# New orders for all engines, one buffer of v and five of x, in a two-layer graph attention kernel

## The chip, the cores and the metric

The kernel runs on one core of a Trainium2 chip. A core has five engines that run side by side, each through its own list of instructions in order: TensorE (PE; its weight loads are shown apart, as PEld), VectorE (DVE), ScalarE (ACT), GpSimd (POOL) and SyncE (SP), which here issues all transfers (DMA). An instruction that needs another engine's result waits on a semaphore, and everything behind it in its engine's list waits too. The metric is the time of one execution on the device, in microseconds (us). The median of three runs of the kernel before is 3153.78 us (3152.27 to 3154.47).

## The reference

The input is 64 graphs of 256 nodes, each node with 512 features, and an adjacency matrix per graph. Two layers follow each other. Both normalise x over the features, apply a relu, compute an attention over the edges of the graph, and add the result to x:

```python
h = jnp.maximum(_layernorm(x, axis=-1), 0.0)
x = x + _L0_gnn_ref(h, adj, ...)     # 8 heads of 64
h = jnp.maximum(_layernorm(x, axis=-1), 0.0)
x = x + _L1_gnn_ref(h, adj, ...)     # one head
```

Layer 0 is attention with queries, keys and values, and a gate:

```python
q, k, v = x @ Wq.T, x @ Wk.T, x @ Wv.T                      # split in 8 heads
scores = where(adj != 0, q @ k.T / 8, -inf)
c = softmax(scores) @ v
gate = sigmoid(concatenate([c, x]) @ Wg.T + bg)
return gate * x + (1 - gate) * c
```

Layer 1 takes its scores from two vectors: `Wh = h @ W`, `e = leaky_relu(Wh @ a1 + (Wh @ a2).T)`, a softmax over the edges, and `elu(softmax(e) @ Wh)`. All is float32.

## The kernel before

Every graph passes through some 190 named steps, and each step issues a few instructions on one engine. The order is written out by hand: `PLAN` gives each step a time within the graph (`sc.0@12.5`), graph g is shifted by g times `ROUND` = 48, `MOVED` holds tables of their own for graphs 0, 1, 2 and the last three, and `ONCE` places the work on the weights. All steps of all graphs are sorted by these times, and the instructions are issued in that order; each engine keeps it. The times themselves decide nothing but the order. Because a graph's steps stretch from about -25 to 161, four graphs are in work at once, and one round of 48 on each engine mixes steps of graph g (queries, keys, values, scores), g-1 (weighing, gate), g-2 and g-3 (layer 1).

Names that the change and the prediction touch, with their lines:

- `product` (L368 on PE, L381 and L385 for the sums): each of the products qk, v, z (the gate) and wh (layer 1) is done by a scheme with seven half-size products instead of eight. Steps `.1` to `.7` are the matmuls, `.u1` to `.u3` partial sums, `.c00` to `.c11` the four quadrants of the result. They need sums of halves of the left side (`Sh`, `Sg`, `Sc`, `S1`, on POOL, L352).
- `sc.0`, `sc.1` (L565): scores of four heads each, two heads at a time on 64 rows of PE; four PSUM banks each. `max.hji` (DVE, L575) adds the mask, writes `e` and its row extreme `low`, and so empties the bank; `exp` (ACT, L585) and `scale` follow, then `turn` (L607), `send`, `fetch`: the transposition of e goes through DRAM.
- `we.hj` (L625) weighs v with e, two heads side by side, into the banks pc; `cT.h` (ACT, L634) copies pc out.
- `po.t` (L802): the product of layer 1. Its bank is read by `pos.t` (ACT, L822), then `neg.t` (DVE, L816); `xn`, `elu` and `add` finish the graph.
- `nm0`, `again` (ACT, L436): the normalising relus; `th`, `sh`, `fh`: the transposition of h through DRAM (DVE L444, SP L452 and L459). Graphs 0 and 1 transpose h on PE instead.
- `w1` in `ONCE`: the two transfers of the weights of layer 1 (L303).

PSUM has 8 banks in one pool (L250). A tile takes a bank that an earlier tile has left, and its first matmul waits until the readers of that tile are done. The order of the steps decides which bank that is. SBUF pools hold a fixed number of buffers for each kind of tile, and work the same way:

```python
    sb = {tag: pool(tag, bufs) for tag, bufs in {
        "x": 4, "mask": 3, "hT": 3, "S": 3, "qk": 2, "v": 2, "wh": 1, "e": 5,
        "cT": 1, "z": 2, "h": 2, "tmp": 5, "U": 3,
    }.items()}
```

Of the kernel before, what the change touches and what calls it, by code (L numbers as in the profile page):

```python
# [23 lines left out]
load@-25.517 st0.0@-25.362 st0.1@-25.032 edges@-22.334 root0@-21.913 nb0@-21.901 nm0.0@-21.307 nm0.1@-20.126  # L24
th.0@-17.618 th.1@-17.305 sh@-14.322 fh@-6.377 Sh.0@-3.038 qk.1@-2.257 Sh.1@-2.212 qk.6@-0.012 v.1@1.071
qk.u1@1.807 qk.u2@2.34 qk.2@2.869 Sh.2@3.73 qk.7@4.792 mask@4.893 qk.c00@6.08 qk.5@6.215 qk.u3@6.435 Sh.3@6.863
qk.c11@7.713 qk.4@8.038 qk.c10@8.845 v.6@9.888 qk.3@10.508 sc.0@12.5 v.u1@13.047 v.u2@13.932 max.000@14.256
max.001@14.568 exp.000@15.12 exp.001@15.307 rec.00@16.501 scale.001@16.56 qk.c01@17.137 max.010@17.753
turn.001@18.015 max.011@18.139 scale.000@18.256 sc.1@18.495 v.7@18.547 v.5@19.32 v.2@19.814 max.101@19.887
exp.010@20.123 exp.011@20.389 max.111@20.411 v.u3@20.681 v.c11@20.959 exp.101@21.371 exp.111@21.858  # L30
max.110@22.149 max.100@22.173 v.3@22.179 v.4@22.277 exp.110@22.423 rec.11@23.42 v.c10@24.24 v.c00@24.916
turn.000@26.369 rec.01@28.756 v.c01@31.638 scale.010@31.798 exp.100@32.951 send.00@33.353 rec.10@35.481
scale.100@38.106 fetch.00@38.826 scale.110@39.168 scale.111@39.248 scale.101@41.535 turn.100@42.016
turn.101@42.558 send.10@43.507 scale.011@43.509 turn.011@44.888 turn.010@45.765 send.01@45.995 Sg.2@46.166
turn.110@47.124 turn.111@49.33 send.11@52.01 fetch.01@56.797 fetch.11@59.033 we.00@61.926 Sg.0@62.715
fetch.10@63.663 we.01@64.269 we.10@64.517 we.11@65.623 cT.1@65.931 cT.0@67.935 tc.0@68.178 tc.1@68.862
z.1@70.621 Sg.1@71.204 again.0@71.805 Sc.0@72.846 sc_c@73.436 again.1@74.487 Sc.1@76.35 fc@76.652 z.6@77.432
Sc.3@77.753 Sg.3@79.038 z.u1@80.986 Sc.2@81.017 z.u2@83.459 plus.0@83.493 z.5@83.895 z.7@84.755 plus.1@85.174
diff.1@85.992 z.u3@87.161 z.c11@88.054 z.u2b@88.325 z.2@89.486 z.c00@89.717 z.c11b@89.726 z.3@89.799 z.4@90.441
tanh.11@90.924 z.c01@91.769 tanh.01@95.639 z.c10@96.01 z.c10b@97.905 tanh.10@98.145 mix.1@98.236 res.1@98.964  # L40
diff.0@99.559 tanh.00@99.951 mix.0@100.406 st1.1@100.781 res.0@100.798 st1.0@100.966 root1@101.973 nb1@102.977
nm1.0@103.141 nm1.1@103.718 th1.0@103.809 th1.1@103.955 sh1@112.184 fh1@115.308 S1.0@115.907 wh.1@116.663
S1.1@117.265 wh.6@118.302 wh.u1@118.466 wh.5@121.753 wh.u2@122.654 S1.2@123.088 S1.3@123.832 wh.7@124.6
wh.2@126.678 wh.u3@127.794 wh.c11@128.831 wh.3@129.585 wh.4@129.976 wh.c01@130.035 ej@130.677 wh.c00@131.651
wh.c10@132.05 lo.0@132.707 lo.1@132.844 lk@133.374 gm@134.11 gx.0@134.576 gx.1@135.087 tg@136.647 gr@138.907
sg@139.411 fg@148.441 po.1@152.197 po.0@152.604 pos.1@152.634 neg.1@152.713 xn.1@153.592 elu.1@153.6
neg.0@154.07 pos.0@156.444 xn.0@157.095 add.1@157.968 elu.0@158.19 add.0@158.822 store.1@161.344 store.0@161.344
# [3 lines left out]
load@-66.492 st0.0@-62.166 st0.1@-41.873 nb0@-40.496 nm0.0@-38.867 nm0.1@-38.355 th.1@-34.404 Sh.0@-26.584  # L51
qk.1@-25.431 edges@-18.94 Sh.1@-17.462 Sh.2@-16.454 qk.u1@-10.175 qk.2@-9.152 qk.c00@-7.78 qk.6@-5.72
qk.u2@-3.448 qk.5@-2.78 mask@0.57 qk.7@1.243 Sh.3@1.626 v.1@2.076 qk.u3@3.139 v.6@4.324 qk.c11@4.336 qk.4@5.375
v.u1@5.993 qk.c10@6.112 qk.3@6.393 Sg.0@7.009 v.u2@7.919 sc.0@8.357 qk.c01@9.423 max.001@12.509 max.000@12.592
exp.001@13.04 sc.1@13.629 max.011@13.907 max.010@14.682 exp.000@15.376 v.2@15.579 rec.00@16.911 v.7@17.36
scale.000@18.711 exp.011@19.032 max.101@19.061 max.110@19.132 turn.000@19.238 exp.010@20.325 rec.01@21.098
scale.001@21.597 v.5@22.024 scale.011@22.79 scale.010@23.067 turn.001@24.046 exp.101@25.554 v.u3@26.692
v.4@27.162 turn.011@27.308 again.1@27.619 max.100@27.777 turn.010@32.196 exp.100@32.343 rec.10@32.984
exp.110@33.128 max.111@34.114 exp.111@34.131 v.c11@35.258 v.c10@35.534 v.3@35.908 scale.100@37.307
turn.100@37.416 send.00@37.59 send.01@37.594 fetch.00@37.81 rec.11@39.483 scale.101@40.086 scale.111@40.147  # L60
turn.101@40.354 scale.110@40.455 Sg.1@40.682 turn.111@40.713 turn.110@41.59 v.c00@45.064 send.10@46.347
send.11@47.204 v.c01@48.602 fetch.01@49.506 fetch.10@51.661 fetch.11@54.488 we.00@60.762 we.01@61.54
we.10@61.569 we.11@63.173 cT.0@64.565 cT.1@64.842 tc.1@66.783 tc.0@67.555 Sc.0@69.612 Sg.3@70.908 sc_c@72.721
z.1@72.817 Sc.1@74.782 Sg.2@74.799 Sc.2@75.418 z.5@78.409 z.u1@78.601 z.6@80.632 z.2@81.279 z.u2@81.896
fc@82.244 again.0@83.023 Sc.3@83.211 z.7@83.889 z.u3@85.445 diff.1@85.474 z.c11@85.865 z.4@86.808 z.c10@87.745
diff.0@87.746 z.c00@87.868 z.c11b@88.24 tanh.11@89.515 z.c10b@90.556 z.3@90.697 tanh.10@90.804 z.u2b@91.332
plus.1@91.418 mix.1@91.555 tanh.00@93.686 res.1@93.921 st1.1@94.842 z.c01@95.935 tanh.01@97.013 plus.0@97.295
mix.0@97.955 res.0@99.045 st1.0@99.639 root1@101.517 nb1@104.33 nm1.1@105.445 nm1.0@105.781 th1.1@106.103
th1.0@106.886 sh1@109.588 fh1@113.042 S1.2@115.324 S1.0@118.555 S1.1@119.128 wh.1@119.447 wh.u1@120.614
wh.5@121.547 wh.6@123.717 wh.2@124.548 wh.u2@125.134 S1.3@125.305 wh.c00@126.073 wh.7@126.229 wh.u3@126.984  # L70
wh.c11@127.33 wh.3@127.662 wh.c01@128.416 wh.4@128.924 ej@129.658 wh.c10@130.963 lo.0@132.107 lo.1@133.497
lk@133.677 gm@134.909 gx.0@135.769 gx.1@136.316 tg@137.119 gr@142.324 sg@144.148 fg@150.305 po.1@152.131
po.0@152.865 neg.1@153.296 pos.1@153.813 xn.1@154.051 elu.1@154.34 neg.0@154.926 add.1@155.869 pos.0@156.073
xn.0@157.112 elu.0@158.192 add.0@159.655 store.1@162.725
""",
    1: """
load@-53.598 st0.0@-44.732 st0.1@-42.689 root0@-41.915 nb0@-40.574 nm0.0@-36.709 nm0.1@-22.87 th.1@-21.253
Sh.2@-20.954 qk.1@-19.381 edges@-18.368 Sh.0@-16.578 Sh.1@-15.935 v.1@-15.77 mask@-15.703 qk.6@-13.279
qk.u1@-10.861 v.6@-8.864 qk.u2@-7.508 qk.5@-5.489 qk.7@-4.754 qk.2@-3.858 qk.c00@1.72 qk.u3@5.331 qk.c11@7.207
Sh.3@7.326 qk.4@7.838 qk.c10@8.486 qk.3@8.97 sc.0@9.079 max.001@9.977 exp.001@10.528 v.u1@11.082 max.000@12.255  # L80
v.u2@12.364 exp.000@13.461 max.011@14.196 max.010@15.765 qk.c01@15.794 sc.1@16.565 rec.00@17.993
scale.000@18.895 scale.001@19.223 v.2@19.942 v.7@20.191 turn.000@23.213 v.5@24.104 turn.001@24.94 send.00@25.481
v.u3@25.507 max.101@26.024 v.4@26.782 v.c11@26.961 v.3@28.971 exp.011@29.35 exp.010@29.396 exp.101@29.983
rec.01@30.852 max.110@30.882 max.100@31.75 Sg.0@32.268 max.111@32.42 exp.100@32.663 v.c01@33.021 exp.110@33.03
exp.111@33.081 rec.10@34.808 rec.11@35.041 v.c10@35.764 scale.011@36.086 scale.010@36.5 scale.111@37.128
turn.010@37.67 scale.100@37.935 scale.110@37.969 v.c00@38.069 Sg.2@38.586 turn.011@38.709 scale.101@39.08
turn.100@39.547 turn.101@40.024 send.01@40.421 turn.111@42.041 turn.110@42.176 fetch.00@42.3 send.11@45.118
fetch.01@48.751 again.0@54.727 again.1@58.028 send.10@59.369 fetch.11@60.182 we.01@60.839 fetch.10@61.056
we.00@64.361 we.10@64.363 we.11@64.622 cT.1@65.84 Sg.1@66.919 cT.0@67.49 tc.1@69.264 tc.0@69.429 z.1@69.839
sc_c@71.013 Sc.0@75.071 Sc.1@75.381 fc@75.545 Sc.3@75.836 z.6@78.559 z.u1@80.518 z.u2@80.535 Sc.2@80.727  # L90
z.2@81.066 z.7@82.757 diff.0@82.831 z.u2b@85.217 z.5@85.437 Sg.3@85.608 z.u3@85.949 z.4@86.212 plus.1@86.287
z.c00@88.083 z.c11@88.484 z.c10@89.655 z.3@90.713 plus.0@91.852 z.c11b@92.08 z.c01@93.718 z.c10b@93.892
tanh.00@95.111 diff.1@96.325 tanh.10@96.948 tanh.11@97.047 tanh.01@98.456 mix.1@100.033 res.1@100.15
mix.0@101.437 st1.1@101.796 res.0@102.261 st1.0@102.536 root1@103.086 nb1@104.102 nm1.0@104.132 th1.0@104.221
# [818 lines left out]
```

## Time and profile before

| | |
|---|---|
| median of three runs | 3153.78 us |
| profiled execution, its own time | 3155.37 us |
| its span on the core | 3153.3 us |
| PE busy | 3123.9 us, 99% |
| DVE, ACT, POOL busy | 77%, 47%, 58% |
| transfers | 593 MB, 188 GB/s |
| one round in the steady stretch (from the transposes of `ej` to the next) | 48.46 us |

The profile is one execution. It names groups of instructions by line and by tiles (out<-in), with their busy time, the mean duration of one, and the idle time of the engine in front of them with what ended it. The timeline merges instructions of a kind that follow each other: the start, the time from the first start to the last end, and the number of instructions; in brackets the idle time in front. A float32 matmul appears as two records. Matmuls overlap, so that the time of a group is better read from its start to the start of the next.

### The profile page before, as it was taken

The numbers are of one execution on the slowest core, as the hardware profiler recorded it, in microseconds if no ns is written. First come the engines' busy times: TensorE is split into PE (matmuls) and PEld (weight loads), VectorE is DVE, ScalarE is ACT, GpSimd is POOL, SyncE is SP. The second block draws the span as 40 slices with busy tenths as digits, with TensorE's granted clock in tenths as the row PEclk, the third lists the DMA queues.
The fourth block names the chain that finished last, engine by engine and source line by source line (L and its number), as shares of the span: only waits on it lengthen the run. The fifth ranks groups of instructions, "written<-read, shape, count | busy, mean of one in ns | idle before, by whom it ended". The sixth has DMA issues, their size and how long they took to land.

```text
span 3153.3 us, 61657 instructions
## 1 busy us (share of the span) xinstructions
PE 3123.9 (99%) x19668; PEld 2729.8 (87%) x19668; DVE 2435.7 (77%) x6310; ACT 1471.4 (47%) x4039; POOL 1836.1 (58%) x2502
## 2 busy tenths in 40 slices
PE   8999999999999999999999999999999999999997
PEld 7888888888888888888888888888888888888886
DVE  7787777777777777777777777777777777777875
ACT  4445445454454454444544544445445444454443
POOL 4566565565665655656656556566565565565654
PEclk9999999999999999999999999999999999999999
DMA  7677777777777777777777777777777777777662
GB/s 218 183 193 187 190 196 189 189 190 192 196 185 189 197 187 188 193 190 196 185 190 194 188 186 197 188 195 186 190 195 186 185 200 188 195 184 194 185 177 86
DMA packets 1107155, 593.19 MB, mean 188 GB/s; under 512 B 687632, under 2 KB 1032720, under 8 KB 1106832
## 3 DMA queue, kind: packets, MB, share of 16 engines
q1 hardware_dynamic: 1106832, 589.25, 72.3%
q8 instruction: 158, 2.59, 0.4%
q14 instruction: 165, 1.35, 0.1%
HBM read 306.45 MB, written 282.59 MB: 187 GB/s over the span
## 4 chain that ended last, share of the span: by engine, by line
PE 95%; DMA 1%; DVE 1%; SPq 1%; POOL 1%; issue 0%; ACT 0%; DVEq 0%; POOLq 0%; ACTq 0%
PE pmb_qk L368 10%; PE pmb_z L368 10%; PE ps L565 8%; PE pma_qk L368 7%; PE pmc_qk L368 7%; PE pc L625 7%; PE pma_z L368 7%; PE po L802 7%; PE pmc_z L368 7%; PE pmb_v L368 5%; PE pmb_wh L368 5%; PE pma_wh L368 3%; PE pmc_wh L368 3%; PE pma_v L368 3%; PE pmc_v L368 3%; PE pe L746 0%
## 5 line engine op out<-in xcount | busy, mean ns | idle before, releaser
L585 ACT ACTIVATE e<-e,low 128x256 f32<-128x256 f32 x1024 | 507.0, 500 | 98.9 <-DVE low L575 89.5
L601 POOL TENSOR_SCALAR e<-e,rec 128x256 f32<-128x256 f32 x768 | 383.6, 516 | 122.3 <-DVE rec L592 122.1
L841 POOL TENSOR_TENSOR x<-x,pos 128x512 f32<-128x512 f32 x126 | 160.9, 1277 | 468.5 <-DVE pos L833 468.5
L575 DVE CUSTOM_DVE_ANT_0 e<-ps,mask 128x256 f32<-128x256 f32 x1024 | 375.2, 414 | 9.7 <-PE ps L565 9.6
L607 DVE STREAM_TRANSPOSE eb<-e 128x512 f32<-128x512 f32 x512 | 345.5, 693 | 8.8 <-ACT e L599 1.2
L436 ACT ACTIVATE h<-x,nb_l,rs_l 128x512 f32<-128x512 f32 x256 | 195.0, 808 | 292.7 <-DVE nb_l L431 266.3
L565 PE MATMUL ps<-qk 64*128 64x256 f32 x2048 | 279.9, 392 | 0.4 <-DVE low L575 0.4
L426 POOL TENSOR_TENSOR rs_l<-ve_l,mhalf 128x2 f32<-128x2 f32 (+1 forms) x129 | 90.6, 702 | 297.1 <-DVE ve_l L422 269.2
L565 PEld LDWEIGHTS ps<-qk 64*128 64x128 f32 x2048 | 204.1, 186 | 57.8 <-DVE low L575 23.1
L802 PE MATMUL po<-wh,egT 128*128 128x256 f32 x1024 | 237.3, 384 | 3.2 <-ACT egT L784 2.9
L625 PE MATMUL pc<-eT,v 128*64 128x256 f32 x2048 | 235.6, 382 | 1.9 <-DMA eT<-there_e 1.8
L802 PEld LDWEIGHTS po<-wh,egT 128*128 128x128 f32 x1024 | 192.5, 193 | 29.8 <-ACT egT L784 3.5
L625 PEld LDWEIGHTS pc<-eT,v 128*64 128x64 f32 x2048 | 141.5, 137 | 88.0 <-issue 22.7
L352 POOL TENSOR_TENSOR S<-h1T 128x256 f32<-128x256 f32 x128 | 93.7, 732 | 202.9 <-DMA h1T<-there_h 126.9
L816 DVE TENSOR_SCALAR neg<-po,rec 128x512 f32<-128x512 f32 x128 | 95.7, 748 | 132.5 <-ACT pos L822 129.6
L585 ACT ACTIVATION_READ_ACCUMULATOR e<-e,low 128x1 f32 x1024 | 195.0, 190 | 0.0
L768 ACT ACTIVATE eg<-eg,nm 128x256 f32<-128x256 f32 x128 | 64.0, 500 | 274.3 <-DVE nm L762 274.3
L822 ACT ACTIVATE pos<-po,rec 128x512 f32<-128x512 f32 x128 | 88.0, 687 | 210.6 <-issue 118.1
L444 DVE STREAM_TRANSPOSE h<-h 128x512 f32<-128x512 f32 x248 | 172.0, 701 | 8.7 <-ACT h L436 3.3
L415 DVE BATCH_NORM_STATS2 bs_l<-x 128x6 f32<-128x512 f32 x256 | 174.4, 681 | 3.8 <-DMA x<-in_x_dram 3.4
L381 DVE TENSOR_TENSOR wh<-pmc_wh,u_wh 128x257 f32<-128x257 f32 x128 | 54.5, 426 | 148.5 <-PE pmc_wh L368 146.4
L673 POOL TENSOR_TENSOR d<-d,c 128x512 f32<-128x512 f32 x128 | 164.4, 1285 | 0.0
(152 smaller groups left out, 8265.6 us busy)
## 6 DMA issues: line engine op xcount, KB each, us to landing
there_e<-eb SPq DMA_DIRECT2D x256, 512.0 KB, 3.3
eT<-there_e SPq DMA_DIRECT2D x1024, 128.0 KB, 3.5
there_h<-h SPq DMA_DIRECT2D x496, 128.0 KB, 3.4
there_c<-cb SPq DMA_DIRECT2D x64, 512.0 KB, 2.9
c<-there_c SPq DMA_DIRECT2D x256, 128.0 KB, 2.9
x<-in_x_dram SPq DMA_DIRECT2D x63, 512.0 KB, 4.3
out_dram<-x SPq DMA_DIRECT2D x63, 512.0 KB, 3.2
hT<-there_h SPq DMA_DIRECT2D x248, 128.0 KB, 3.2
```

The source lines that it names most:

```text
L368: nc.tensor.matmul(s[name, key][(slice(None), *cols)], lhsT, rhs, start=first and i == 0, stop=last and i == len(mms) - 1, skip_group_chec ...
L415: nc.vector.bn_stats(bs, s["x"][:, t, :])
L436: nc.scalar.activation(out, s["x"][:, t, :], AF.Relu, bias=s["nb", layer][:, t:t + 1], scale=s["rs", layer][:, t:t + 1])
L444: nc.vector.transpose(h, h)
L565: nc.tensor.matmul(s["ps", half, jj, i][:, t, :], qk[r:r + DK, 0, jj, t * P:(t + 1) * P], qk[r:r + DK, 1, jj, :], start=True, stop=True,)
L575: nc.vector.tensor_tensor_reduce(e[:, i, t, :], s["ps", half, jj, i][:, t, :], s["mask"][:, t, :], -SCALE, HUGE, ALU.add, ALU.min, accum_o ...
L585: nc.scalar.activation(e, e, AF.Exp, bias=s["low", half][:, jj, i, t:t + 1], scale=-1.0, accum_out=sums[:, jj, i, t:t + 1])
L601: nc.gpsimd.tensor_scalar(e, e, rec, 1.0, ALU.mult, ALU.mult)
L607: nc.vector.transpose(eb[:, :, 4 * i:4 * i + 4, :].rearrange("p b n c -> p n b c"), e)
L625: nc.tensor.matmul(pc[i * DK:(i + 1) * DK, jj, :].rearrange("p (t a c) -> p t a c", t=NT, c=32), s["v"][:, kc, hd * DK:(hd + 1) * DK], s[" ...
L673: nc.gpsimd.tensor_tensor(d, d, s["c"][t], ALU.subtract)
L802: nc.tensor.matmul(po[:, n, :], s["egT"][:, t, kc, :], to_wh(s, g, kc, n)[:, :HH], start=(kc, n) == (0, 0), stop=(kc, n) == (NT - 1, 1), s ...
```

## The change

The times in `PLAN`, in the six tables of `MOVED` and in `ONCE` are all rewritten, so the order of the steps is another one on every engine; no step is added or taken away. The pool of v has one buffer in place of two, that of x five in place of four.

On PE, a steady round before has the order qk.4, po.1, po.0, v.6, qk.3, sc.0, we.00, we.01, we.10, we.11, sc.1, v.7, v.5, v.2, wh.1 and so on. After, it is qk.4, po.0, qk.3, v.7, v.2, po.1, sc.0, we.01, we.00, we.10, we.11, sc.1, v.3, v.4, wh.1. On DVE, around the scores: before max.000, max.001, rec.00, qk.c01, max.010, turn.001, max.011, max.101, tc.0; after neg.0, qk.c01, nb0, elu.0, neg.1, max.011, max.010, th.1, v.u3, elu.1, max.000, v.c11, th.0, max.001, max.110. On ACT: before xn.0, exp.000, exp.001, cT.1, cT.0, exp.010, exp.011; after pos.1, xn.1, nm0.1, again.0, nm0.0, cT.0, exp.010, cT.1, exp.000, exp.011.

```diff
 PLAN = """
-load@-25.517 st0.0@-25.362 st0.1@-25.032 edges@-22.334 root0@-21.913 nb0@-21.901 nm0.0@-21.307 nm0.1@-20.126
...
-qk.c11@7.713 qk.4@8.038 qk.c10@8.845 v.6@9.888 qk.3@10.508 sc.0@12.5 v.u1@13.047 v.u2@13.932 max.000@14.256
-max.001@14.568 exp.000@15.12 exp.001@15.307 rec.00@16.501 scale.001@16.56 qk.c01@17.137 max.010@17.753
-turn.001@18.015 max.011@18.139 scale.000@18.256 sc.1@18.495 v.7@18.547 v.5@19.32 v.2@19.814 max.101@19.887
...
-sg@139.411 fg@148.441 po.1@152.197 po.0@152.604 pos.1@152.634 neg.1@152.713 xn.1@153.592 elu.1@153.6
...
+load@-50.672 st0.0@-48.955 st0.1@-47.821 root0@-38.184 nb0@-37.123 nm0.1@-29.56 nm0.0@-28.012 th.1@-27.761
...
+v.7@10.9 v.2@10.953 qk.c00@12.201 sc.0@14.892 max.011@16.85 max.010@18.632 v.u3@21.472 exp.010@22.747
+max.000@23.034 v.c11@23.409 max.001@24.188 sc.1@24.213 exp.000@24.365 exp.011@24.661 v.3@24.788 max.110@24.806
...
+lk@135.599 gm@135.616 gx.1@140.75 gx.0@141.02 tg@141.763 sg@143.83 gr@152.036 fg@153.077 po.0@153.781
+pos.0@153.792 neg.0@153.922 xn.0@156.41 elu.0@157.474 po.1@158.645 add.0@158.767 pos.1@159.243 neg.1@160.27
...
 ONCE = """
-wgc@10.917 wgh@19.432 sumgc.0@42.007 sumgc.2@42.137 sumgc.1@42.313 sumgh.0@47.029 sumgh.2@53.384 sumgh.1@54.715
-sumgc.3@55.21 small@64.212 sumgh.3@73.845 w1@84.687 edge.20@91.004 edge.30@93.277 edge.21@97.801 edge.31@97.88
...
+sumgc.3@67.553 sumgc.2@67.566 w1@71.651 edge.10@73.258 sumgh.3@73.871 edge.01@74.38 edge.00@75.742
...
-        "x": 4, "mask": 3, "hT": 3, "S": 3, "qk": 2, "v": 2, "wh": 1, "e": 5,
+        "x": 5, "mask": 3, "hT": 3, "S": 3, "qk": 2, "v": 1, "wh": 1, "e": 5,
```

On SP, the head had fetch.11/0, load/2, sc_c/0, send.00/1, edges/2, fc/0, sh/2, w1, fh/2 (step/graph); after, load/2 comes in the first transfers, and the order is fetch.01/0, w1, sh/2, fh/2, sc_c/0, fc/0. In the steady round the last fetch of e, fetch.11, now follows sh1 of the graph before.

## The prediction

> **What bounds the kernel now.** I read the page first, then the waits by engine, then the timeline of one round in the steady stretch, then the timeline of the first 100 us. The engine table says that TensorE (PE) is busy for 99% of the span, so no engine that gets faster can help unless PE itself stands still somewhere.
>
> ```profile
> PE 3123.9 (99%) x19668; PEld 2729.8 (87%) x19668; DVE 2435.7 (77%) x6310; ACT 1471.4 (47%) x4039; POOL 1836.1 (58%) x2502
> L565 PEld LDWEIGHTS ps<-qk 64*128 64x128 f32 x2048 | 204.1, 186 | 57.8 <-DVE low L575 23.1
> ```
>
> The row to see is the second. PE's matmul row hides short waits, because matmuls overlap; the weight loader (PEld) does not. It stood 23.1 us before the score matmuls, until VectorE (DVE) had written `low`. The list of waits says in how many pieces, and what else PE waited for:
>
> ```profile
> PEld ps L565 <- DVE low L575: 23.1, 59, 0.6
> PE pma_qk L368 <- DMA hT<-there_h: 5.2, 1, 5.2
> PE ptr L782 <- ACT eg L768: 3.5, 1, 3.5
> ```
>
> 59 waits in 64 graphs: one per round, 0.39 us each. The other two are single waits, one in the head, one in the tail. Now one steady round, all engines:
>
> ```profile
> 1640.34 3.63 PE L802 MATMUL po<-wh,egT 128*128 128x256 f32 x16
> 1642.32 0.69 ACT L822 ACTIVATE pos<-po,rec 128x512 f32<-128x512 f32 x1 [2.10 <-issue]
> 1643.04 0.75 DVE L816 TENSOR_SCALAR neg<-po,rec 128x512 f32<-128x512 f32 x1 [2.08 <-ACT pos L822]
> 1643.83 0.63 ACT L826 ACTIVATE neg<-neg 128x512 f32<-128x512 f32 x1 [0.82 <-DVE neg L816]
> ...
> 1646.54 2.00 PE L565 MATMUL ps<-qk 64*128 64x256 f32 x16
> ...
> 1648.47 3.67 PE L625 MATMUL pc<-eT,v 128*64 128x256 f32 x32
> ...
> 1652.07 2.01 PEld L565 LDWEIGHTS ps<-qk 64*128 64x128 f32 x16 [0.39 <-DVE low L575]
> 1652.07 2.41 PE L565 MATMUL ps<-qk 64*128 64x256 f32 x16
> 1652.19 1.07 ACT L634 COPY cT<-pc 128x512 f32<-128x512 f32 x2 [1.65 <-PE pc L625]
> ```
>
> The first group of 16 score matmuls (sc.0) takes 2.00 us, the second (sc.1, the same work) 2.41. sc.1 needs four PSUM banks; the last one is that of max.011, which DVE empties last (its two reductions start at 1652.55 and 1652.87). From its start to that of the next group, sc.0 takes 1.93 us and sc.1 2.34: 0.41 us lost. That the round pays it in full can be seen early on: the two rounds where sc.1 starts at 198.82 and 247.00 lose 0.13 and 0.20 there, and last 48.18 and 48.25 us; the steady ones lose 0.41 and last 48.46. In the head:
>
> ```profile
> 73.16 1.03 PE L368 MATMUL pmc_z<-wgc_sb,Sc 128*128 128x256 f32 x4
> 79.41 2.05 PE L368 MATMUL pma_qk<-hT,wq_sb 128*128 128x128 f32 x8 [5.23 <-DMA hT<-there_h]
> 81.25 1.92 PE L368 MATMUL pma_qk<-hT,wk_sb 128*128 128x128 f32 x8
> 82.96 1.25 PE L368 MATMUL pma_v<-wv_sb,hT 128*128 128x256 f32 x4
> ```
>
> hT of graph 2 comes 5.23 us late: the two halves of W1 (w1, issued at 66.57) stand in SP's queue between that graph's `sh` and `fh`, and land 8.5 and 9.9 us after issue. After the wait PE runs at about half speed for 16 matmuls: 82.96 - 79.41 = 3.55 us, against 2 x 0.89 for the same in any later round, so 1.8 more.
>
> **The change, part by part.** The work is the same, matmul for matmul, and PE changes between the score, weighing and full-width forms about as often (262 changes in the order as built, 261 before), so PE's own sum moves by nothing. What can move is its waiting.
>
> *sc.1 (the main term).* In the built order sc.1's four banks are now those emptied by max.010, cT.0 (the copy of the first half of pc), max.000 and cT.1; max.011 and max.010 come first on DVE, and max.001's bank is not needed before wh.1, 3.6 us later. So the last bank hangs on ScalarE (ACT). I follow that chain with the rows above, from T, the start of the weighing matmuls. po.1 now stands directly ahead of sc.0. po's last matmul starts 0.22 + 0.09 + 1.93 = 2.24 before T and takes 0.38, so po.1 ends at T-1.86. After po, pos starts 0.09 later and takes 0.69; neg starts 0.03 later and takes 0.75; its exponential starts 0.04 later: T-0.27. ACT then issues, start to start: that exponential 0.54 (0.636 less 0.09 overlap), three normalising relus at 0.72 (0.81 less 0.09), cT.0 at 0.48, exp.010's two halves at 0.49: cT.1 starts at T+3.89 (pc is done at T+3.7, so ACT is what is late), takes 0.59, and a load follows its releaser by 0.05: T+4.53. sc.1 starts at T+3.60, so that load stands 0.93 after the group's start. In the rounds named above this load stood at 1.00, 1.07 and 1.28 after the start and cost 0.13, 0.20 and 0.41: cost = lateness past 0.87. So 0.06 us is left of 0.41. The other banks have more room: cT.0 ends at T+3.0 for a use at T+3.6; max.000 ends after max.011, max.010 (4 x 0.345), th.1 0.62, v.u3 0.33, elu.1 0.62 and 2 x 0.345 at T+3.7, for a load at T+4.36. Bounds: nothing left (0), or as much as now (0.41). I take 0.06 over 58 rounds, 3.5 us: the gain is 23.1 - 3.5 = 19.6.
>
> *The bank of pc's first half* is now the one of po.1, the group just before sc.0. By the same chain neg.1 ends at T-0.31: 0.3 us to spare, no cost. In front of neg.1 on DVE stand elu.0 and, through the buffer that neg reuses, add.0 on POOL (1.28): po.0, pos.0, neg.0, its exponential, elu.0 and add.0 take 0.09 + 0.69 + 0.03 + 0.75 + 0.04 + 0.63 + 0.70 + 1.28 = 4.2 us after po.0 ends, and neg.1 can start no earlier than 6.0 after it (qk.3, v.7, v.2 and po.1 on PE: 1.79 + 2 x 0.86 + 1.73 = 5.2, and pos.1): 1.8 to spare, some 1 us if DVE's qk.c01 (0.66) gets in between. Bounds: 0 to 0.7 us per round, if one DVE operation of 0.70 gets in front.
>
> *One buffer of v.* The first write of the next v (v.c11, 0.41) now has to wait for the last weighing matmul, about T+3.7; DVE comes to it behind max.000 at T+3.7, so it waits for nothing. Queued behind it are th.0 and max.001, whose bank is wanted 1.9 us after max.001 ends (T+5.4 against T+7.3). Cost 0, bounds 0 and 0.34 per round (one v copy less its overlap). The Trainium skill, "Trainium Kernel Development and Optimization", section Best Practices, says to double-buffer for performance, and so speaks against this part; going by it, that upper bound would be booked, 0.34 x 60 = 20 us, and would eat the whole gain. The row behind it, 1.9 us of cover, decides for me.
>
> *A fifth x* lets load and the statistics run a graph earlier (before, x is issued at 1652.70, takes 4.25 us to land and is read at 1658.23): 0, nothing that PE waits for hangs on x in the steady stretch.
>
> *SP's queue.* The last fetch of eT now stands behind sh1, four issues of 0.74 = 3.0 us. Before, the last fetch is issued at 1688.6, lands 3.5 later and is used at 1698.6: 6.5 spare, of which 3.5 are left. sh and fh move ahead likewise. Cost 0; upper bound one late fetch, some 0.5 us a round.
>
> *POOL and the sums.* Sg, Sc, S1, Sh move ahead of the products that read them; PE waits for POOL only in the tail now (0.6), so 0 either way.
>
> *Head.* w1 is issued ahead of graph 2's sh, right behind graph 0's last fetch, about 47 us; by its own rows it has landed by 57, and sh and fh of graph 2 no longer have it between them: their 3.4 and 3.2 us to landing fit before 74.0, where PE came to wait. The 5.2 and the 1.8 us go: 7.0 (bounds 0 and 7). Late next would be graph 2's first sums on POOL, two of 0.76 after the landing.
>
> *New starts and ends.* The orders of graphs 0 to 2 and 61 to 63 are all new. Such rounds now show single bank waits of 0.6 and 0.9 us (near 147 and 152), and the tail 12 us of waits that follow from the chain of the last graph (softmax, transposition, product), which is no shorter after. I book +3, between -3 and +8.
>
> Sum: 19.6 + 7.0 - 3 = 23.6 us less. The profiled execution took 3155.37 (span 3153.3 and 2.1 around it), 1.6 above the median of 3153.78; its 23.6 taken from the median give **3130**.
>
> **Rivals.** (1) *The wait moves instead of going*: the ACT chain ends 0.2 to 0.35 later than worked out (one of the relus held, or exp.010 later), and sc.1 keeps 0.25 to 0.41. For it: the chain is ten operations long with 0.06 missing. Against: each has a steady duration. Gain 23.1 - 58 x (0.25 to 0.41), so 0 to 9, and 4 from head and edges: 3141 to 3150. (2) *Slower*: neg.1 on DVE ends later than T, because something of 0.70 stands before it or add.0 is late. Every 0.1 us beyond the 0.3 spare costs 0.1 at pc and, through its exponential and ACT, another 0.1 at sc.1: 11.6 us in 58 rounds. It decides from about 0.2 beyond the spare; with a whole DVE operation (0.4 beyond) the sum is 23.6 - 46, so 23 slower: 3177. For it: po has been moved right up to sc.0, where before v.6 and qk.3 stood between (2.7 us). Against: nothing in DVE's order stands between. (3) *The wait never cost anything*, the round being bound elsewhere: against it stand the three round lengths; only the head's 7 less 3 would be left, 3150. (4) *All goes, and the edges gain 3*: 3153.8 - 23.1 - 7 - 3 = 3121.
>
> **How the numbers follow.** Forecast 0.55, its own range 3122 to 3138; (4) 0.14; (1) 0.18; (2) 0.08; (3) 0.05. Leaving out the slower case and the upper end of (1) and (3) gives 3118 to 3148. What a measurement of this kernel can tell from no change is 0.2%, 6.3 us: faster by more is below 3147.5, which is the forecast, (4) and most of (1): 0.84. Within: the rest of (1), most of (3): 0.09. Slower: 0.07.
>
> **What would show it.** Right: sc.1 within 0.1 us of sc.0, PEld's wait for `low` gone, rounds of 48.1 us, no wait for hT in the head. Wrong: PEld waiting before ps for ACT cT, or before pc for DVE neg; rounds of 48.4 or more; or new waits for eT and hT in the steady stretch.

## The result and the profile after

The changed kernel takes **3135.73 us** (median of 4 runs, 3133.86 to 3136.5) against 3153.62 of the kernel before in the same job: a ratio of 0.9943, 95% interval 0.9926 to 0.996. The forecast of 3130 lay 5.7 below, and the time is inside the forecast's own range of 3122 to 3138. The profiled execution took 3136.5, span 3134.63, 18.6 less than the 3153.26 of before. Line numbers are one higher than before from the pools on (L565 is now L566).

The page of the kernel after, engine table and costliest groups:

```profile
PE 3104.0 (99%) x19668; PEld 2708.9 (86%) x19668; DVE 2465.1 (79%) x6310; ACT 1458.2 (47%) x4039; POOL 1818.2 (58%) x2502
L566 PE MATMUL ps<-qk 64*128 64x256 f32 x2048 | 257.7, 390 | 0.5 <-ACT neg L827 0.5
L566 PEld LDWEIGHTS ps<-qk 64*128 64x128 f32 x2048 | 192.0, 186 | 60.0 <-DVE low L576 22.9
```

The same group of matmuls on the page of the kernel before, a row that the prediction does not show:

```profile
L565 PE MATMUL ps<-qk 64*128 64x256 f32 x2048 | 279.9, 392 | 0.4 <-DVE low L575 0.4
```

Here is the first surprise. The third row of the first fence still says 22.9 us of waiting for `low`, where the prediction led with 23.1 and expected 3.5 to be left. By that row nothing has happened. But PE's *busy* time on the same matmuls fell from 279.9 to 257.7, by 22.2 us. The loss that the change removed stood in the busy column. The list of PEld's waits after the change shows what the idle row is (columns: what was waited for, us in total, times, longest):

```profile
PEld ps L566 <- DVE low L576: 22.9, 60, 0.5
PEld ps L566 <- issue: 20.3, 61, 0.4
PEld pmc_v L369 <- DVE low L576: 19.2, 58, 0.3
PEld pc L626 <- DVE neg L817: 18.6, 56, 0.3
```

In this kernel every entry into another form of matmul (two heads on 64 rows for `ps`, two on 64 columns for `pc`, full width for `pmc_v`) shows a gap of 0.33 to 0.39 us on the weight loader, once a round, whatever releaser is named, `issue` (no releaser) included; between groups of the same form it is 0.03. It goes with the change of form, and the name beside it is merely that of the last semaphore. Its size is not the same everywhere: the entry into sc.0 shows 0.12 in the kernel before, where qk.3 stands ahead of it with matmuls of 128 columns, and 0.33 after, where po.1 stands there with 256.

One steady round after the change, timeline of all engines (start, duration, engine):

```profile
1639.59 1.60 PEld L566 LDWEIGHTS ps<-qk 64*128 64x128 f32 x16 [0.33 <-issue]
1639.59 2.00 PE L566 MATMUL ps<-qk 64*128 64x256 f32 x16
1639.70 0.69 ACT L823 ACTIVATE pos<-po,rec 128x512 f32<-128x512 f32 x1 [2.85 <-PE po L803]
1640.49 0.75 DVE L817 TENSOR_SCALAR neg<-po,rec 128x512 f32<-128x512 f32 x1 [2.89 <-ACT pos L823]
1641.27 0.63 ACT L827 ACTIVATE neg<-neg 128x512 f32<-128x512 f32 x1 [0.89 <-DVE neg L817]
...
1641.52 3.67 PE L626 MATMUL pc<-eT,v 128*64 128x256 f32 x32
1643.93 0.57 ACT L635 COPY cT<-pc 128x512 f32<-128x512 f32 x1
1645.12 1.61 PEld L566 LDWEIGHTS ps<-qk 64*128 64x128 f32 x16 [0.39 <-DVE low L576]
1645.12 2.02 PE L566 MATMUL ps<-qk 64*128 64x256 f32 x16
1645.39 0.57 ACT L635 COPY cT<-pc 128x512 f32<-128x512 f32 x1
```

sc.1 (1645.12) lasts 2.02 and not 2.41, though the 0.39 of idle time in front of it is exactly that of before. From its start to the start of the next group it takes 1.944 us in the median round (before: 2.337; sc.0: 1.927): 0.017 is left of 0.41, where the forecast left 0.06. With T = 1641.52 the chain falls nearly where the prediction put it: pos at T-1.82 (put at T-1.77), neg at T-1.03 (T-1.05), its exponential at T-0.25 (T-0.27), cT.0 at T+2.41 (T+2.43), cT.1 at T+3.87 (T+3.89).

Where the 18.6 us of span come from, measured between the starts of step `ej`, one per round:

| stretch | before | after | difference | forecast |
|---|---|---|---|---|
| start to first ej | 118.86 | 113.83 | -5.0 | -7.0 |
| rounds 1 to 4 | 47.8, 48.18, 48.25, 48.46 | 48.95, 46.32, 48.05, **55.42** | +6.05 | +3 for all starts and ends |
| 53 steady rounds | 48.46 each | 48.07 each | -20.8 | -19.6 (for 58 rounds) |
| last six rounds, last ej to end | | | +1.1 | in the +3 |

### The profile page after: what moved, and what is told of

The parts are those of the page before. It is cut to its first block, busy times and chain, and to the rows that moved or that the text cites. A ratio compares the mean times of both kernels' runs of the same rounds, so it can differ in the third digit from the quotient of the medians.

```text
span 3134.6 us, 61537 instructions
## 1 busy us (share of the span) xinstructions
PE 3104.0 (99%) x19668; PEld 2708.9 (86%) x19668; DVE 2465.1 (79%) x6310; ACT 1458.2 (47%) x4039; POOL 1818.2 (58%) x2502
## 4 chain that ended last, share of the span: by engine, by line
PE 96%; DVE 2%; DMA 1%; issue 0%; ACT 0%; SPq 0%; POOL 0%; DVEq 0%; ACTq 0%
PE pmb_qk L369 11%; PE pmb_z L369 10%; PE ps L566 8%; PE pc L626 7%; PE pmc_qk L369 7%; PE po L803 7%; PE pma_z L369 7%; PE pma_qk L369 7%; PE pmc_z L369 7%; PE pmb_wh L369 5%; PE pmb_v L369 5%; PE pmc_v L369 4%; PE pmc_wh L369 3%; PE pma_wh L369 3%; PE pma_v L369 3%
## 5 line engine op out<-in xcount | busy, mean ns | idle before, releaser
L602 POOL TENSOR_SCALAR e<-e,rec 128x256 f32<-128x256 f32 x768 | 354.7, 482 | 24.9 <-DVE rec L593 20.7
L608 DVE STREAM_TRANSPOSE eb<-e 128x512 f32<-128x512 f32 x512 | 336.1, 684 | 6.4 <-DMA there_e<-eb 5.7
L566 PE MATMUL ps<-qk 64*128 64x256 f32 x2048 | 257.7, 390 | 0.5 <-ACT neg L827 0.5
L803 PE MATMUL po<-wh,egT 128*128 128x256 f32 x1024 | 245.8, 383 | 4.3 <-DMA egT<-there_g 2.5
L566 PEld LDWEIGHTS ps<-qk 64*128 64x128 f32 x2048 | 192.0, 186 | 60.0 <-DVE low L576 22.9
L684 ACT ACTIVATE z<-z 128x256 f32<-128x256 f32 x256 | 93.5, 409 | 309.5 <-POOL z L391 190.3
L803 PEld LDWEIGHTS po<-wh,egT 128*128 128x128 f32 x1024 | 192.0, 193 | 30.2 <-DMA egT<-there_g 2.9
L626 PEld LDWEIGHTS pc<-eT,v 128*64 128x64 f32 x2048 | 141.1, 137 | 86.3 <-DVE neg L817 18.6
L679 POOL TENSOR_TENSOR x<-x,c 128x512 f32<-128x512 f32 x128 | 200.3, 1565 | 0.0
L391 POOL TENSOR_TENSOR z<-z,bias 128x256 f32<-128x256 f32 x128 | 90.6, 727 | 168.3 <-DVE z L382 168.2
```

Of the source, the lines that this page charges most:

```text
L566: nc.tensor.matmul(s["ps", half, jj, i][:, t, :], qk[r:r + DK, 0, jj, t * P:(t + 1) * P], qk[r:r + DK, 1, jj, :], start=True, stop=True,)
L602: nc.gpsimd.tensor_scalar(e, e, rec, 1.0, ALU.mult, ALU.mult)
L608: nc.vector.transpose(eb[:, :, 4 * i:4 * i + 4, :].rearrange("p b n c -> p n b c"), e)
L626: nc.tensor.matmul(pc[i * DK:(i + 1) * DK, jj, :].rearrange("p (t a c) -> p t a c", t=NT, c=32), s["v"][:, kc, hd * DK:(hd + 1) * DK], s[" ...
L679: nc.gpsimd.tensor_tensor(xt, xt, s["c"][t], ALU.add)
L803: nc.tensor.matmul(po[:, n, :], s["egT"][:, t, kc, :], to_wh(s, g, kc, n)[:, :HH], start=(kc, n) == (0, 0), stop=(kc, n) == (NT - 1, 1), s ...
```

## The experiments

**One swap on DVE, nothing else.** In the kernel before, `turn.001`, a transposition of e for the heads before, stood ahead of `max.011`, whose bank sc.1 waits for. One number of PLAN is changed:

```diff
-turn.001@18.015 max.011@18.139
+turn.001@18.2 max.011@18.139
```

> The kernel before, with one entry of the plan moved: turn.001 goes behind max.011 on DVE, so that max.011, which empties the last bank of sc.1, ends 0.62 us earlier. Theory A (the steady gain is the 0.41 us that sc.1 loses inside its group, and the round pays it in full): sc.1 shrinks from 2.34 to about 1.93 us start to start, the round from 48.46 to 48.05, the time by about 0.41 x 57 = 23 us, to about 3130. Theory B (the gain of the changed kernel needs its whole new order, the sums further ahead on POOL and DVE): the round stays above 48.3 and the time above 3145. Side test: if the 23.1 us that the list of waits put on DVE low is that loss, its row goes; if that row is the gap at the entry of the group, it stays at some 20 us under one name or another.

Measured: 3134.84 (3132.06 to 3135.58), ratio 0.9938 [0.9924, 0.9953]. sc.1 takes 1.928 us, the steady rounds are 48.05. The page of this run beside its list of PEld's waits:

```profile
L565 PE MATMUL ps<-qk 64*128 64x256 f32 x2048 | 256.5, 389 | 0.2 <-DVE low L575 0.2
```

```profile
PEld ps L565 <- DVE low L575: 22.5, 58, 0.6
```

So one transposition of 0.7 us in the wrong place in DVE's list was the whole loss inside sc.1, and moving it alone gives as much time as the rewriting of all orders. It also settles the reading of the rows: the loss is gone and the idle row stays at 22.5. The time lies 4.8 above theory A's 3130; eight rounds of this run last 0.14 to 1.4 us longer than 48.05, 4.5 us in all. PE's timeline in the longest of them:

```profile
684.73 1.10 PE L368 MATMUL pma_wh<-w_sb,h1T 128*128 128x257 f32 x4 [1.14 <-DMA h1T<-there_h]
```

In six of the eight, PE's weight loader stands 0.3 to 1.5 us before this first product of layer 1 and starts 0.1 to 0.2 us after h1T, the transposed input, has landed (the list of waits puts these six down to ACT, once more a name only); in the other two it stands 0.4 and 0.6 us before the next product, for POOL's sums of h1T. In the steady rounds h1T lands 0.1 to 1.6 us ahead of that product in the kernel before, and 3.0 to 4.7 us ahead in the changed kernel, whose 53 steady rounds have none of these waits. That margin is what the new order has over the one swap. Why h1T comes late in just these rounds stays open.

**The pools alone.** In the kernel before:

```diff
-        "x": 4, "mask": 3, "hT": 3, "S": 3, "qk": 2, "v": 2, "wh": 1, "e": 5,
+        "x": 5, "mask": 3, "hT": 3, "S": 3, "qk": 2, "v": 1, "wh": 1, "e": 5,
```

> The kernel before with the pools alone changed: one buffer of v, five of x, all orders as before. Theory A (v's first write comes behind the last weighing matmul on DVE anyway): no difference, 3152 to 3156, rounds of 48.46. Rival (the second buffer of v is worth something): every round longer by up to 0.34 us, up to 3175.

Measured: 3154.58 (3152.4 to 3156.53), ratio 1.0002 [0.9993, 1.0012], rounds of 48.46 as before. Giving up a buffer of v costs nothing in this order, and neither does a fifth x bring anything. The prediction set against this part the advice to double-buffer (Trainium skill, "Trainium Kernel Development and Optimization", Best Practices) and an upper bound of 20 us. The page gives as its aim to "Overlap DMA with compute"; v is written by DVE and ACT and not by a transfer, so this run does not test the page's advice. It shows that the 20 us are not there. The other way round, two buffers of v within the changed order, was not tried.

**The price of a late bank.** In the changed kernel, `exp.011` is put ahead of cT.1 on ACT, so that sc.1's last bank comes 0.98 us later:

```diff
-max.001@24.188 sc.1@24.213 exp.000@24.365 exp.011@24.661
+max.001@24.188 sc.1@24.213 exp.000@24.365 exp.011@23.3
```

> The changed kernel with exp.011 ahead of cT.1 on ACT (one entry of PLAN). Tests the price by which the forecast was made: cost of sc.1 = lateness of its last bank's load past 0.87 us after the group's start. Both halves of exp.011 take 0.98 us of ACT, so cT.1, and with it that load, comes 0.98 later, at about 1.87 after the start. Theory A: sc.1 from start to next start 1.94 + about 0.98 = 2.92 us, rounds of 49.0 instead of 48.07, 55 rounds: about +54, 3190 (3183 to 3197). Theory B (PE's group can be held without the round paying, or the held matmuls are overtaken): less than half, below 3162.

Measured: 3187.99 (3187.45 to 3192.18), 52 more than the changed kernel. The timeline around sc.1, and the waits of PEld in this run:

```profile
1671.13 1.16 PEld L566 LDWEIGHTS ps<-qk 64*128 64x128 f32 x10 [0.39 <-DVE low L576]
1671.13 1.56 PE L566 MATMUL ps<-qk 64*128 64x256 f32 x10
...
1672.39 0.57 ACT L635 COPY cT<-pc 128x512 f32<-128x512 f32 x1
...
1673.01 0.73 PEld L566 LDWEIGHTS ps<-qk 64*128 64x128 f32 x6 [0.72 <-ACT cT L635]
1673.01 1.13 PE L566 MATMUL ps<-qk 64*128 64x256 f32 x6 [0.31 <-ACT cT L635]
```

```profile
PEld ps L566 <- ACT cT L635: 39.5, 57, 0.7
PEld ps L566 <- DVE low L576: 22.8, 59, 0.5
PEld ps L566 <- issue: 20.7, 62, 0.4
```

The late load stands 1.87 us after the group's start; less 0.87 that is 1.00, and sc.1 takes 2.930, 1.00 more than sc.0. In the changed kernel the same load stands at 0.888, and 0.017 is lost. The price "lateness past 0.87" holds over a span of 1 us, and the round pays it in full (49.05 against 48.07). A real wait looks like this: a row of its own that was not there before, of 0.69 us x 57, inside the group, while the 22.8 beside it has not moved. And even here the row understates: 39.5 us of idle time where these groups got 55 us longer (178.5 against 123.5 in sum), because the load of the other head of the pair goes on alone meanwhile and counts as busy.

**The slower rival, on purpose.** In the changed kernel `neg.1` goes behind the two reductions of `max.011` on DVE:

```diff
-po.1@158.645 add.0@158.767 pos.1@159.243 neg.1@160.27
+po.1@158.645 add.0@158.767 pos.1@159.243 neg.1@161.0
```

> The changed kernel with neg.1 behind max.011 on DVE (one entry of PLAN): the slower rival's mechanism made on purpose. neg.1 starts at about 1642.33 in place of 1640.49 of the steady round, 1.84 later, that is 1.55 beyond its spare of 0.3. Theory A (the price as the forecast put it: every 0.1 beyond the spare costs 0.1 at pc and another 0.1 at sc.1): 3.1 us a round, rounds of 51.2, about +175, 3310. Theory B (sc.1's chain is counted from pc's own start; once pc is held, the chain on ACT is late only against a pc that is late itself, so sc.1 loses at most the spare of 0.3 more): pc held about 1.55, sc.1 about 2.2 to 2.3 us long, 1.85 a round, rounds of 49.9, about +103, 3239 (3225 to 3250).

Measured: 3234.39 (3234.18 to 3237.21), rounds of 49.90. Timeline:

```profile
1640.67 2.00 PE L566 MATMUL ps<-qk 64*128 64x256 f32 x16
...
1643.41 0.74 DVE L817 TENSOR_SCALAR neg<-po,rec 128x512 f32<-128x512 f32 x1
1643.54 3.22 PEld L626 LDWEIGHTS pc<-eT,v 128*64 128x64 f32 x32 [1.28 <-DVE low L576]
...
1648.91 0.73 PEld L566 LDWEIGHTS ps<-qk 64*128 64x128 f32 x6 [0.61 <-ACT cT L635]
```

neg.1 is 1.84 us later against sc.0 than in the changed kernel, and the round is 1.83 us longer (49.90 against 48.07), not 3.1: the prediction's price for its slower rival, 0.1 at pc and 0.1 more at sc.1 for each 0.1, counted one delay twice. The size of theory B is right and its split is wrong. pc is held 0.95 and sc.1 0.89, not 1.55 and 0.3, because with the new order pc's first bank is no longer that of po.1: pc starts at 1643.54, before neg.1 has ended, right behind the second reduction of max.011. The order of the readers had dealt the banks anew. So the spare of 0.3 us at that bank was not itself tested.

**The 55.42 us round.** In the table of graph 2 in the changed kernel, `elu.1` stands at 175.908, while it is at 166.01 in PLAN. The waits of SP's queue between 235 and 290 us, and PE's waits in the round that follows:

```profile
SPq L491 <- DVE pos L834: 11.4, 1, 11.4
```

```profile
264.60 1.13 PE L369 MATMUL pma_qk<-hT,wq_sb 128*128 128x128 f32 x8 [1.90 <-DMA hT<-there_h]
...
277.52 1.13 PE L369 MATMUL pmb_qk<-Sh,wq_t 128*128 128x128 f32 x8 [1.19 <-DVE u_qk L382]
...
284.45 1.16 PE L369 MATMUL pmb_qk<-hT,wq_t 128*128 128x128 f32 x8 [2.26 <-DVE u_qk L382]
```

The load of the adjacency of graph 6 (L491) stands 11.4 us at the head of SP's queue until elu.1 (DVE, L834) gives back a buffer of the pool `tmp`; sh and fh of that round stand behind it, and PE waits for hT and then for what follows from it. Undone:

```diff
-xn.0@158.042 elu.0@158.613 pos.1@159.906 neg.1@159.936 add.0@162.097 xn.1@163.951 elu.1@175.908 add.1@180.211
+xn.0@158.042 elu.0@158.613 pos.1@159.906 neg.1@159.936 add.0@162.097 xn.1@163.951 elu.1@166.01 add.1@180.211
```

> The changed kernel, with one entry of graph 2's own table moved: elu.1 at 166.01, where the plan of the other graphs has it, in place of 175.908. In the changed kernel the adjacency load of graph 6 stands 11.4 us in SP's queue until that elu.1 gives its buffer back, and the transfers of h behind it come late. Theory A (that is the cause of the 55.42 us round): the round falls to between 48 and 49.5 and the time by 6 to 7.4 us, to about 3129. Rival (the round is slow because four differently ordered graphs meet there, and another late transfer takes its place): less than 3 us.

Measured: 3129.67 (3127.82 to 3130.79), 6.1 less than the changed kernel; the round is 48.86, and the 11.4 us of SP are gone. One entry had given back a quarter of the gain.

**The head: w1 alone, in two places.** First w1 of the kernel before was moved to the place in SP's queue that it was thought to have after the change, right behind graph 0's last fetch:

```diff
-sumgc.3@55.21 small@64.212 sumgh.3@73.845 w1@84.687
+sumgc.3@55.21 small@64.212 sumgh.3@73.845 w1@54.6
```

> The kernel before, with w1 alone moved: its two transfers are issued right behind the last fetch of graph 0, ahead of sh of graph 2. Theory A: the wait of 5.23 us for hT of graph 2 and the 1.8 us at half speed behind it go, 5 to 7 us less: 3147 to 3149. Rival: hT of graph 2 is late for another reason as well (load of graph 2, the transposes behind the scores of graph 1), and 3 us or less are gained: 3151 or more.

Measured: 3155.43 (3154.07 to 3157.0), ratio 1.0007 [0.9998, 1.0016]. The 5.23 us for hT went, and nothing came of it. DVE's timeline of this run shows what is late in its stead:

```profile
57.39 0.69 DVE L415 BATCH_NORM_STATS2 bs_l<-x 128x6 f32<-128x512 f32 x1 [2.84 <-DMA x<-in_x_dram]
...
63.06 0.38 DVE L381 TENSOR_TENSOR u_v<-pmb_v,u_v 128x256 f32<-128x256 f32 x1
```

In that order graph 2's x is issued right behind w1. It lands 8.9 us after issue in place of 5.5, DVE stands 2.84 us for it, and the partial sums of PE's products queue behind: u_v comes at 63.06, before at 59.47 (0.7 of these 3.6 us are from the start of this execution, whose first product comes at 10.32 against 9.30). PE stands for u_v and then for v, and behind these waits its clock is low:

```profile
63.50 1.13 PE L368 MATMUL pmb_v<-wv_t,hT 128*128 128x256 f32 x4 [2.38 <-DVE u_v L381]
65.49 2.07 PE L368 MATMUL pmc_v<-wv_sb,Sh 128*128 128x256 f32 x4 [0.86 <-DVE v L381]
```

The granted clock of TensorE is 0.66 on average between 65 and 70 us of this run, and the product that takes 2.07 us here takes 1.13 in the kernel before; by 69 us PE is 1.4 us further behind. The half speed that the prediction read behind the wait for hT is the same thing: there the granted clock is 0.66 from 75 to 85 us, and 1.00 in the changed kernel. The changed kernel issues no x between 36 and 69 us. So w1 was moved again, to right behind graph 2's x and the small weights:

```diff
-small@64.212 sumgh.3@73.845 w1@84.687
+small@64.212 sumgh.3@73.845 w1@64.3
```

> The kernel before with one entry moved: the two issues of w1 stand in SP's queue right behind graph 2's x, a_sb and bias, at about 49 us, not ahead of x as in the run that gained nothing. There DVE stood 2.84 us for that x, landing 8.9 us after issue in place of 5.5, and all its later work with it. Theory A (w1 between sh and fh of graph 2 costs what PE lost there, and the other place only made x late): x lands about 5.5 after issue as before, PE's wait of 5.23 for hT and the half speed behind it go, no new wait on DVE near 57 us, the first ej about 7 earlier (112), 3146.8 +-1.5. Theory B (the wait for hT costs little because PE would be held by DVE a few us later anyway): the hT wait goes, waits for u_v, v, Sh or u_qk between 60 and 95 us take its place, first ej 117 to 119, 3151 to 3154.

Measured: 3150.59 (3149.99 to 3152.6), ratio 0.9989 [0.9981, 0.9998]; x is on time. PE's timeline of the head:

```profile
75.07 1.13 PE L368 MATMUL pma_qk<-hT,wq_sb 128*128 128x128 f32 x8 [0.48 <-DMA hT<-there_h]
...
78.35 1.16 PE L368 MATMUL pmb_qk<-Sh,wq_t 128*128 128x128 f32 x8 [0.39 <-POOL Sh L352]
...
84.33 1.13 PE L368 MATMUL pmb_qk<-Sh,wq_t 128*128 128x128 f32 x8 [1.27 <-DVE u_qk L381]
```

The first ej comes 4.0 earlier (114.83), between theory A (7) and theory B (0 to 2). Of the 7.0 us that PE lost at the wait for hT, other waits just behind it (0.48, 0.39 and 1.27 here) take back 2.1, and this execution stood 0.4 behind the other before it came there (first product at 10.07 against 9.30); the last 0.4 are not accounted for. The half speed is gone: the granted clock is 1.00 from 60 to 90 us. Heads of one kernel differ between executions: in the runs with turn.001 alone and with the pools alone, whose heads have the orders of the kernel before, PE stands 3.77 and 4.02 us for hT, and the first ej is at 118.17 and 118.28. A difference at the first ej is good to some 0.7 us.

**The first products.** In the kernel with elu.1 mended, the sum over Wq, which waits for its weights, is also moved behind graph 0's first transposed h on DVE:

```diff
-wq@-73.553 wk@-69.272 sumq.0@-68.556 wake@-47.401
+wq@-73.553 wk@-69.272 sumq.0@-44.0 wake@-47.401
```

> The changed kernel with two entries moved: elu.1 of graph 2 back to the place that it has in all other graphs (3129.7 alone), and sumq.0 behind graph 0's th on DVE, so that the first matmuls don't wait 1.21 us for hT behind a sum that waits for Wq. Theory A (the head's first wait is on the path): first ej about 1 us earlier than 113.8, 3128.6 (3127 to 3130). Theory B (Wq's own landing or u_qk holds PE a little later anyway): 3129.7, no different from elu.1 alone.

Measured: 3129.63 (3129.13 to 3130.76), no different from 3129.67. The first product starts 1.0 us earlier (9.41 against 10.45), waits 1.66 for another weight's sum right behind, and the first ej stands at 113.27 against 113.15. So that wait is not on the path, within the 0.7 us by which heads differ.

**The two edits that gained in the kernel before, together.** turn.001 at 18.2 and w1 at 64.3, the two diffs above:

> The kernel before with the two edits that gained singly put together: turn.001 behind max.011 on DVE (3134.84 alone) and w1 right behind graph 2's x, a_sb and bias in SP's queue (3150.59 alone, first ej at 114.8). Theory A (the two gains lie in different stretches, steady rounds and head, and add): first ej at about 114.8, steady rounds of 48.05, 3134.84 - 3.2 = 3131.6 (3130 to 3133.5). Theory B (w1's earlier landing is lost again in the first rounds, once those are shorter): 3134 to 3135.

Measured: **3128.32** (3128.01 to 3129.7), ratio 0.9917 [0.9904, 0.9931]: the lowest median of these runs, with two numbers changed, and not distinguishable from the changed kernel with elu.1 mended (0.9923 [0.9908, 0.9938]). The first ej is at 114.16 and the rounds are 48.05, as theory A has it, but the time is 1.7 below its range. The profiled spans differ by 5.0 from the run with turn.001 alone, of which 4.0 lie in the head and 0.9 in the rounds (five irregular ones, 2.6 us, in place of eight; all five have the wait at layer 1's first product). The rest of the 6.5 between the medians is about the spread of that earlier run (3132.06 to 3135.58), and is not explained further.

## Why the prediction was right, and where it was not

- **sc.1, main term: right in mechanism, 19.6 forecast for 58 rounds, 20.8 measured over 53 (0.34 and 0.39 a round).** The bank chain through ACT, its times to 0.05 us, and the price past 0.87 all hold (the run with exp.011). But the step that *sized* the term failed: "It stood 23.1 us before the score matmuls, until VectorE (DVE) had written `low`" and "59 waits in 64 graphs: one per round, 0.39 us each". That row is the gap at the change of form, which stands at 22.9 after the change. The loss was inside the group, 2.337 against 1.927, and it showed as 22.2 us of PE busy time. Each matmul is as long as before (median 376 ns in both traces); when the second head's load comes late, the two heads of a pair run less side by side, and busy time grows. 23.1 and 53 x 0.41 = 21.7 lie close by chance. The sentence that the weight loader does not hide waits fell with it: its busy time fell too, from 204.1 to 192.0. So did one of the four signs of being right, "PEld's wait for `low` gone"; the other three came (sc.1 within 0.02 us of sc.0, rounds of 48.07, no wait for hT in the head). Had the size been taken from the group lengths that the prediction also quotes, (0.41 - 0.06) x 58 = 20.3 would have come out, and from the right evidence.
- **pc's bank and neg.1: cost 0, right.** pc takes 3.604 us from start to next start in the steady rounds. The price set for the slower rival was double what the run with neg.1 moved shows.
- **One buffer of v, a fifth x: 0, right** (the run with the pools alone, and rounds of 48.07 in the changed kernel, where v's buffer is single).
- **SP's queue: 0 in the steady rounds, right; wrong at the start.** (The last fetch of eT, issued at 1688.6, landed 3.95 us later in the trace of before, not 3.5, so 6.1 were spare and not 6.5; it decides nothing.) The prediction asked of SP's order only whether fetches come late, not what an issue in it waits for. The adjacency's load waited for a `tmp` buffer and held all behind it.
- **Head: 7.0 forecast, 5.0 measured, and 4.0 for w1 alone.** Both waits went, as said, but the step "The 5.2 and the 1.8 us go: 7.0" failed: a wait that ends is worth only the distance to the next one. How the 5.0 of the changed kernel, whose whole head is new, divide among its edits was not tested. The second fault is that moving w1 was taken as one edit; what it passes in the queue (x of graph 2) decides whether it gains anything.
- **Starts and ends: +3 forecast, +7.2 measured**, inside the bounds of -3 to +8. In the span 18.6 came where 23.6 were forecast: 2.0 short in the head, 4.2 at the starts and ends, 1.2 more in the rounds. One entry accounts for 6.1 of it. The own tables of graphs 0 to 2 were quoted as "all new" and not read step by step against PLAN; elu.1 ten units late in one of them could have been seen.
- **The rivals.** (1), sc.1 keeping 0.25 to 0.41: 0.017 is left. (2), neg.1 late: it did not occur; made on purpose it costs its lateness once. (3), the wait never cost anything: refuted by the one swap, 18.9 us less (3134.84 against 3153.75 in the same job). (4), edges that gain 3: they lost 7.

## What to carry to other kernels

Judge a stall on a pipelined engine by the distance from a group's start to the next group's start against the same work elsewhere in the trace, and only then look for the row that names it: idle time beside a releaser's name can be a gap that goes with a change of form, and a real stall can hide in the busy column of an engine that is "99% busy". Before booking the removal of a wait, ask what stands next behind it, and read in every queue that a step passes what the passed and the passing ones wait for. When a rewritten order gains, try its smallest part alone: here one swap gave the whole gain inside sc.1, and two entries beat the whole as it was built.

## What the runs showed of the hardware that was not expected

- In the steady rounds of the changed kernel the weight loader stands 0.33 us at each change between score, weighing and full-width matmuls, and 0.38 to 0.39 from weighing to scores, also with no releaser behind it (`issue`, 61 times, 20.3 us). In the kernel before it is 0.12 from qk.3 (128 columns) to scores. What the gap costs in time no run shows.
- The granted clock averaged 0.66 from 75 to 85 us in the kernel before, around the end of PE's wait of 5.23 us, and 0.66 from 65 to 70 us in the run with w1 at 54.6, behind waits of 2.38 and 0.86 us. Groups of matmuls that take 1.1 us elsewhere took 1.9 to 2.1 there.
- Of a group of paired matmuls on two halves of PE's rows, a late load costs nothing up to 0.87 us after the group's start where the bank is that of the fifth pair, and one for one beyond (0.888, 1.28 and 1.87 gave 0.017, 0.41 and 1.00).
- Two transfers of 512 KB issued just ahead of another made that one land 8.9 us after its issue in place of 5.5.
